# Layer 0's routed experts on 32-token tiles, four experts side by side in the array, with their weights copied to a fixed tile; context LayerNorm scaled on the vector engine

## The chip, the core and the metric

The kernel is one program on one core of a Trainium2 chip. The core has five engines that run their own instruction queues in order and wait for one another by semaphores: TensorE (PE in the profile, with its weight loads as PEld), VectorE (DVE), ScalarE (ACT), GpSimd (POOL) and SyncE (SP, which here only issues DMAs). The metric is the device time of one execution in microseconds; less is better. Times of several executions are given as a median.

## The reference, cut to what matters

The program is a decoder of four layers over `x` of shape (4, 256, 128), which is 1024 tokens of width 128. Each layer adds a self attention, a cross attention to a context of (4, 512, 128), and a feed-forward part. The change touches layer 0's feed-forward part, a mixture of 32 experts with one expert for each token, beside one shared expert:

```python
x = hidden_states.reshape(-1, h)
shared_out = _swiglu(x, shared_gate_w, shared_up_w, shared_down_w)
logits = x @ gate_w
topk_ids = jnp.argmax(logits, axis=-1)
topk_val = jnp.max(logits, axis=-1)
scores = jax.nn.sigmoid(topk_val)[:, None]
xs = x * scores
tokens_per_expert = jnp.zeros((E,), jnp.int32).at[topk_ids].add(1)      # E = 32
order = jnp.argsort(topk_ids)
sorted_x = xs[order]
g = _grouped_mm(sorted_x, routed_gate_w, tokens_per_expert)             # 128 -> 256
u = _grouped_mm(sorted_x, routed_up_w, tokens_per_expert)               # 128 -> 256
d = _grouped_mm(jax.nn.silu(g) * u, routed_down_w, tokens_per_expert)   # 256 -> 128
routed_out = d[inv]
return (shared_out + routed_out).reshape(b, s, h)
```

Layers 1 and 2 have mixtures too (8 experts, two for each token, hidden width 512), and layer 3 an ordinary feed-forward part. Layer 0's cross attention uses the context after a LayerNorm without gains; that LayerNorm is the other thing that the change touches. The inputs are random, with fixed shapes; all arithmetic of the experts is in f32.

## The kernel before

Tokens stand 128 to a tile, eight tiles in all (`NT`), with the tokens on the partitions.

**Layer 0's attention** is woven by a planner that spreads the steps of one unit (a batch and a kind of attention) over the steps of its neighbours. Beside each cross attention unit it places `normalise_context`, which normalises two tiles of the context `cn` at a time. The statistics are taken by DVE (`st`, `mv`, lines L290 and L291), the reciprocal root by POOL (`ve`, `rs`, L296 and L298), and the scaling `(x - mean) * rs` (L304) by POOL too, because `normalise` is called with `G`.

**A mixture** sorts the tokens by expert without sorting them. `blocks_of` counts the tokens of each expert, rounds each count up to whole blocks, and derives three things: `index`, the slot of each token; `token`, the token of each slot; and `at`, for each block, the column at which its expert's weights begin. Every block has 128 slots and one expert. Since each of the 32 experts may leave one block partly empty, the program reserves `size = k * NT + n_e - 1` blocks, which is 8 + 31 = 39 in layer 0 and 16 + 7 = 23 in layers 1 and 2.

`mixture` then runs over the blocks, with four steps that are one block apart:

- `fetch(b)` gathers the 128 rows of block b from DRAM with an indirect DMA on POOL (L1022), five blocks ahead.
- `rows_T(b)` turns them on TensorE (L1029), and ACT copies them to `xbT` (L1031).
- `hidden(b)` multiplies them with the gate and up weights of the block's expert, 512 columns, one f32 matmul that the profile shows as two records (L1042). ACT takes the silu of the gate half (L1136, `sg`), and DVE multiplies it with the up half (L1137, `h`).
- `turned(b)` turns the 256 hidden columns in two transposes (L1052), and DVE copies them to `hT` (L1054).
- `result(b)` multiplies with the down weights in two matmuls of 128 columns, four records (L1063). After every fourth block ACT copies the sums to `ys` (L1078), and SP writes them to `done` in DRAM.

All weights of all experts lie in SBUF (`e0h`: 128 x 16384, and `e0d`: 128 x 8192). TensorE reads them at an address from a register, which its own queue loads from `at` (L1015) ahead of the matmul:

```python
at_h = offset(0, b, (n_e - 1) * n1)
...
T.matmul(p, lhsT=xbT[b], rhs=wh[:, bass.ds(at_h + 512 * i, 512)], ...)
```

The lines are written in the order hidden(b), rows_T(b + 1), fetch(b + 5), turned(b - 1), result(b - 2); a scheduler places them on each engine's queue, and the engines follow that queue strictly.

In `ffn0` the routing comes first (`next(work)`), then the shared expert in two halves of 512 tokens (L1160 gate and up, L1166 silu to `sgs`, L1167 product to `hTs`, L1171 down, L1176 residual), then the block loop. The scheduler mixes the shared expert's matmuls into the routing. After the loop, layer 1 begins with keys for its strided attention (L1268, L1287), while the routed rows are gathered back (L1106) and added to `x` (L1116).

Of the kernel before, what the change touches and what calls it, by code (L numbers as in the profile page):

```python
# [32 lines left out]
P = 128  # L33
# [150 lines left out]
def decoder(ctx: ExitStack, tc: tile.TileContext, dr, out):  # L184
# [78 lines left out]
    slots = const.tile([32, 8], F32, tag="slots", name="slots")  # L263
    V.tensor_scalar(slots, iota[:32, :8], float(P), None, ALU.mult)
    halves = const.tile([P, 2], F32, tag="halves", name="halves")
    G.memset(halves, -0.5)

# [581 lines left out]

    def all_normalised_T(pool, keep=None, tag="pt"):
        xnT = pool.tile([P, NT * P], F32, tag="xnT", name="xnT", bufs=1)
        for b in range(B):
            normalised_T(b, pool, dst=xnT[:, b * S : (b + 1) * S], keep=keep, tag=tag)
        return xnT
# [29 lines left out]
            hot.append(oh)  # L886
        return mx, hot

    def blocks_of(pool, hots, size, widths):

# [23 lines left out]
            )  # L914
        cs = small.tile([32, 1], F32, tag="cs", name="cs")[:n_e]
        V.tensor_copy(cs, count)
        nb = small.tile([32, 8], F32, tag="nb", name="nb")[:n_e]
        V.tensor_scalar(nb, slots[:n_e], cs, None, ALU.is_lt)
        V.tensor_reduce(cs, nb, AX.X, ALU.add)
        nbb = small.tile([32, P], BF16, tag="nbb", name="nbb")[:n_e]  # L920
        V.tensor_scalar(nbb, onesb[:n_e], cs, None, ALU.mult)
# [1 line left out]
        cum = ps("t")[:, :64]  # L923
        T.matmul(cum, lhsT=nbb, rhs=upto_bf[:n_e], start=True, stop=True)
        base = small.tile([P, 32], F32, tag="base", name="base")[:, :n_e]
        V.tensor_scalar(base, cum[:, :n_e], float(P), None, ALU.mult)
        to = pool.tile([P, n, n_e], F32, tag="to", name="to", bufs=1)
        V.tensor_tensor(
            to, rank.rearrange("p (t e) -> p t e", t=n),
# [47 lines left out]
        for i in range(n_w):  # L977
            T.transpose(xp[:1, i * P : (i + 1) * P], ex[:, i : i + 1], ident)
        fill(4, "g")
        at = pool.tile([1, n_w, P], I32, tag="at", name="at", bufs=1)  # L980
        V.tensor_copy(at, xp[:1, : n_w * P].rearrange("p (i b) -> p i b", i=n_w))
        return index, token, at


# [8 lines left out]
        if fetched:  # L993
            fetched.pop(0)()

    def mixture(pool, n_e, hots, weights, rows_, wh, wd, activate, biases=None):

        k = len(hots)  # L1000
        size = k * NT + n_e - 1
        n1, n2 = wh.shape[1] // n_e, wd.shape[1] // n_e
        nh = n2 // P
        sent = dram.tile([NT * P, D], F32, tag=f"sent{n_e}{k}", name="sent")
        done = dram.tile([size * P, D], F32, tag=f"done{n_e}{k}", name="done")
        nc.sync.dma_start(sent.rearrange("(t p) d -> p t d", p=P), rows_)
        index, token, at = blocks_of(pool, hots, size, (n1, n2) if biases is None else (n1, n2, P))
# [5 lines left out]
        def offset(i, b, most):  # L1013

            return nc.values_load(  # L1015
                at[0:1, i, b : b + 1], engines=[mybir.EngineType.PE], min_val=0, max_val=most,
                skip_runtime_bounds_check_because="an expert's number, limited to the last one's",
            )

        def fetch(b):  # L1020
            xb[b] = pool.tile([P, D], F32, tag="xb", name="xb", bufs=ahead + 1)
            G.indirect_dma_start(  # L1022
                out=xb[b], out_offset=None, in_=sent[:, :],
                in_offset=bass.IndirectOffsetOnAxis(ap=token[:, b : b + 1], axis=0),
            )
# [6 lines left out]

        def hidden(b):
            o = [ps("g") for _ in range(0, n1, 512)]
            at_h = offset(0, b, (n_e - 1) * n1)
            for i, p in enumerate(o):
                if biases is not None:
                    T.matmul(
                        p, lhsT=onesb[0:3, :], rhs=biases[0:3, bass.ds(at_h, 512)],
                        start=True, stop=False,  # L1040
                    )
                T.matmul(  # L1042
                    p, lhsT=xbT[b], rhs=wh[:, bass.ds(at_h + 512 * i, 512)],
                    start=biases is None, stop=True,
                )
            h[b] = pool.tile([P, n2], F32, tag="h", name="h", bufs=3)
            activate(pool, h[b], o)

# [7 lines left out]
        def result(b):  # L1056
            g, i = b // 4, b % 4
            if i == 0:
                y[g] = ps("y")
            cols = slice(i * P, (i + 1) * P)  # L1060
            at_d = offset(1, b, (n_e - 1) * n2)
            for c in range(nh):
                T.matmul(  # L1063
                    y[g][:, cols], lhsT=hT[b][:, c * P : (c + 1) * P],
                    rhs=wd[:, bass.ds(at_d + c * P, P)],
                    start=c == 0, stop=c == nh - 1 and biases is None,
                )
            if biases is not None:
                at_b = offset(2, b, (n_e - 1) * P)
                T.matmul(  # L1070
                    y[g][:, cols], lhsT=onesb[0:3, :],
                    rhs=biases[0:3, bass.ds(at_b + n_e * n1, P)],
                    start=False, stop=True,
                )
            if b == groups[g][-1]:
                n = len(groups[g])
                ys = pool.tile([P, 4, D], F32, tag="ys", name="ys")
                A.copy(ys[:, :n, :], y[g][:, : n * P].rearrange("p (n d) -> p n d", n=n))  # L1078
                nc.sync.dma_start(
                    done[4 * g * P : (4 * g + n) * P, :].rearrange("(n p) d -> p n d", p=P),  # L1080
                    ys[:, :n, :],
                )

        yield
        for b in range(ahead):
            fetch(b)
        rows_T(0)
        for b in range(size + 2):
            if b < size:
                hidden(b)  # L1090
            if b + 1 < size:
                rows_T(b + 1)
            if b + ahead < size:
                fetch(b + ahead)
            if 1 <= b <= size:
                turned(b - 1)
            if b >= 2:
                result(b - 2)
# [41 lines left out]
    def ffn0(wh):  # L1140
        with ExitStack() as st:
            pool = expert_pools(st, "ffn0")
            wd = load("e0d", pool=pool)
            xn = pool.tile([P, NT, D], F32, tag="xna", name="xna", bufs=1)
            xnT = all_normalised_T(pool, keep=[xn[:, t, :] for t in range(NT)], tag="t")
            mx, (hot,) = top(pool, logits_of(pool, xnT, gates[:, 0:32], 32, tag="t"), 1)
            score = pool.tile([P, NT], F32, tag="score", name="score", bufs=1)
            A.activation(score, mx[:, :, 0], AF.Sigmoid)
            for t in range(NT):
                G.tensor_scalar(xn[:, t, :], xn[:, t, :], score[:, t : t + 1], None, ALU.mult)  # L1150
            work = mixture(pool, 32, [hot], None, xn, wh, wd, gated(256))
            next(work)

            for c in range(2):
                hT = pool.tile([P, 2, 512], F32, tag="hTs", name="hTs", bufs=1)
                for ic in range(2):
                    gu = []
# [24 lines left out]
    def ffn1(wh, wd, ahead):  # L1182
        with ExitStack() as st:
# [6 lines left out]
            work = mixture(pool, 8, hots, small_softmax(pool, mx), xn, wh, wd, gated(512))  # L1190
            next(work)
            next(work)
            wq3.extend(ternary_weights(ahead, w3f))
# [13 lines left out]
    def ffn2():  # L1207
        with ExitStack() as st:
# [30 lines left out]
            def activate(pool_, h, o):  # L1239
# [4 lines left out]
                    V.tensor_scalar(h, o[0], 0.0, None, ALU.max)  # L1244

            work = mixture(
                pool, 8, hots, [best[:, i] for i in range(2)], xn, wh, wd, activate, bias
            )
            next(work)
            next(work)  # L1250
# [811 lines left out]
```

## Time and profile before

| what | value |
|---|---|
| median of the three runs | 1609.93 us |
| the three runs | 1610.73, 1606.98, 1609.93 us |
| the profiled execution, its own time | 1610.05 us |
| its span, from first to last instruction | 1608.2 us |
| mean granted clock of TensorE | 0.916 of full speed |
| busy share of the span: PE, DVE, ACT, POOL | 86%, 51%, 45%, 19% |
| chain of work that ended last: PE, DVE, ACT, POOL | 72%, 11%, 7%, 4% |
| hidden matmuls of the three mixtures in that chain (L1042) | 7% |

The shares are averages over stages that have different limits, so a stage is read from its own stretch. Layer 0's attention runs from the start to about 278 us, the routing and the shared expert to about 307 us, the block loop of layer 0 from 309 to 387 us, and layer 1 follows. In the groups of instructions the first number after the bar is the busy time in us, the second the mean duration of one in ns, and after the next bar stands the time that the engine was idle just before them and who ended it. A clock of 1.00 is full speed.

### The profile page before, as it was taken

The page shows a single profiled execution, that of the slowest core. Times are in us where ns is not written, and L with a number is a line of the kernel's source. Part 1 is how long each engine was busy: PE and PEld are TensorE (multiplying, and loading weights), DVE is VectorE, ACT ScalarE, POOL GpSimd, SP SyncE. Part 2 cuts the span into 40 slices and gives each one's busy share as a digit, 9 for nine tenths or more (in the row PEclk, how much of TensorE's full clock was granted, in tenths as well). Part 3 has the DMA queues.
Part 4 walks back from the last instruction along what each step waited for, and adds up shares of the span by engine and source line. Part 5 has one row for each costly group of instructions (what it writes and reads, how often), then busy time and mean ns, then how long its engine had stood idle before and what let it go on. Part 6 is the DMA issues. An engine that isn't in the chain of part 4 may idle for free.

```text
span 1608.2 us, 27001 instructions
## 1 busy us (share of the span) xinstructions
PE 1383.7 (86%) x10108; PEld 733.2 (46%) x10108; DVE 816.0 (51%) x2690; ACT 721.6 (45%) x1428; POOL 312.5 (19%) x440
## 2 busy tenths in 40 slices
PE   4998998698786899888999999999596699999963
PEld 3543333465344465645455554455364344333321
DVE  5676661444564344764434543441433557765336
ACT  0544656233652334256666756766121044344431
POOL 5235100452312224200000000000232522211000
PEclk8999999798798899999999999999698599999985
DMA  8000001232040314150110000000312000000000
GB/s 313 1 1 1 2 1 54 84 68 57 7 202 14 105 39 150 53 183 14 49 45 14 27 1 1 1 1 1 130 45 52 27 1 2 1 2 1 1 2 12
DMA packets 38754, 70.98 MB, mean 44 GB/s; under 512 B 5477, under 2 KB 22159, under 8 KB 36703
## 3 DMA queue, kind: packets, MB, share of 16 engines
q1 hardware_dynamic: 33474, 51.39, 9.1%
q0 software_dynamic: 4000, 8.20, 2.5%
q10 hardware_dynamic: 1152, 9.67, 1.5%
q8 instruction: 82, 1.34, 0.3%
q14 instruction: 46, 0.38, 0.1%
HBM read 51.06 MB, written 18.18 MB: 43 GB/s over the span
## 4 chain that ended last, share of the span: by engine, by line
PE 72%; DVE 11%; ACT 7%; POOL 4%; issue 3%; DMA 2%; another core or an unknown queue 0%; SPq 0%; ACTq 0%; POOLq 0%; DVEq 0%
PE s L538 7%; PE g L1042 7%; PE o L574 7%; PE s L473 6%; PE o L1789 6%; PE s L1769 5%; PE f L1718 4%; PE y L1063 4%; PE s L525 3%; PE f L1704 2%; PE s L532 2%; PE t L1052 2%; PE f L1674 2%; DVE mx L480 2%; PE s L1762 2%
## 5 line engine op out<-in xcount | busy, mean ns | idle before, releaser
L473 PE MATMUL s<-kc,qm 32*128 32x256 f32 (+1 forms) x1024 | 217.3, 559 | 14.0 <-POOL qm L428 8.4
L555 ACT ACTIVATE pr<-s 128x512 f32<-128x512 f32 x256 | 137.9, 596 | 185.1 <-PE s L538 183.6
L538 PE MATMUL s<-qm,kc 32*128 32x512 f32 (+1 forms) x896 | 207.5, 605 | 0.0
L296 POOL TENSOR_SCALAR ve<-mv 128x2 f32<-128x2 f32 (+1 forms) x56 | 12.7, 228 | 758.4 <-DVE mv L291 694.1
L1729 ACT ACTIVATE ss<-ss,ntop 128x768 f32<-128x768 f32 x128 | 118.6, 928 | 85.6 <-DVE ntop L1727 85.3
L480 DVE TENSOR_REDUCE mx<-s 128x1 f32<-128x512 f32 (+1 forms) x192 | 122.5, 685 | 65.2 <-PE s L538 50.5
L574 PE MATMUL o<-pr,v 128*32 128x256 f32 (+1 forms) x1792 | 145.6, 391 | 9.0 <-ACT os L580 4.1
L1723 DVE CUSTOM_DVE_ANT_0 ss<-f,n 128x512 f32<-128x512 f32 x128 | 83.4, 689 | 74.5 <-PE f L1718 74.3
L473 PEld LDWEIGHTS s<-kc,qm 32*128 32x128 f32 x1024 | 88.1, 204 | 68.9 <-issue 19.5
L484 DVE CUSTOM_DVE_ANT_0 junk<-s,nmif 128x512 bf16<-128x512 f32 x128 | 83.0, 688 | 54.0 <-PE s L473 53.5
L1789 PE MATMUL o<-pr,v 128*64 128x256 f32 x768 | 108.8, 395 | 0.0
L1022 POOL DMA_INDIRECT xb<-sent,token x85 | 81.0, 952 | 140.5 <-PE t L1029 63.8
L557 ACT ACTIVATE pr<-s,n 128x512 f32<-128x512 f32 x128 | 80.1, 690 | 60.4 <-PE s L538 40.1
L1769 PE MATMUL s<-qT,kT 64*128 64x256 f32 x768 | 105.3, 390 | 0.0
L574 PEld LDWEIGHTS o<-pr,v 128*32 128x32 f32 x1792 | 40.4, 109 | 117.5 <-issue 88.6
L1776 ACT ACTIVATE pr<-s,n 128x512 f32<-128x512 f32 x128 | 80.2, 678 | 22.0 <-PE s L1769 21.9
L428 POOL TENSOR_SCALAR qm<-q,consts 128x256 f32<-128x256 f32 x64 | 58.6, 932 | 145.9 <-ACT q L425 115.6
L532 PE MATMUL s<-mT,selg 12*128 12x256 bf16 x768 | 80.6, 276 | 4.2 <-DVE mT L274 1.2
L1054 DVE COPY hT<-t 128x512 f32<-128x512 f32 (+1 forms) x85 | 48.1, 566 | 68.8 <-PE t L1052 64.3
L1711 DVE CUSTOM_DVE_ANT_0 ss<-f,nought 128x256 f32<-128x256 f32 x128 | 46.8, 421 | 60.9 <-PE f L1704 60.7
L1718 PE MATMUL f<-kT,qT 64*128 64x512 f32 x256 | 76.6, 624 | 0.1
L1789 PEld LDWEIGHTS o<-pr,v 128*64 128x64 f32 x768 | 47.8, 136 | 60.4 <-issue 23.5
(404 smaller groups left out, 2513.8 us busy)
## 6 DMA issues: line engine op xcount, KB each, us to landing
e0h<-in_e0h SPq DMA_DIRECT2D x8, 1024.0 KB
kd<-ahead SPq DMA_DIRECT2D x20, 256.0 KB
vd<-ahead SPq DMA_DIRECT2D x20, 256.0 KB
kT<-kd SPq DMA_DIRECT2D x20, 256.0 KB
v<-vd SPq DMA_DIRECT2D x5, 1024.0 KB
done<-ys SPq DMA_DIRECT2D x19, 256.0 KB
e0d<-in_e0d SPq DMA_DIRECT2D x1, 4096.0 KB
e1h<-in_e1h ACTq DMA_DIRECT2D x1, 4096.0 KB
```

Source lines behind the costliest of these rows:

```text
L473: T.matmul(sc[:, i, :], lhsT=u.qm[r, g + i, qt * P : (qt + 1) * P], rhs=u.kc[r, :], start=u.row_mask is None, stop=True,)
L480: V.tensor_reduce(u.mx[:, qt, j, g : g + per], sc, AX.X, ALU.max)
L532: T.matmul(sc[:, i, :], lhsT=selg[r, gp + i, :], rhs=u.mT[r, :], start=u.cols_mask is None and i == 0, stop=False,)
L538: T.matmul(sc, lhsT=u.kc[r, kt * P : (kt + 1) * P], rhs=u.qm[r, gp : gp + 2, first:], start=u.clip, stop=True,)
L555: A.activation(dst, sc, AF.Exp)
L574: T.matmul(u.po[gp][32 * j : 32 * j + 32, i, first:], lhsT=u.v[:, kt, 4 * j + gp + i, :], rhs=u.pr[gp, kt, j][:, i, first:], start=kt + i ...
L1042: T.matmul(p, lhsT=xbT[b], rhs=wh[:, bass.ds(at_h + 512 * i, 512)], start=biases is None, stop=True,)
L1718: T.matmul(sc[h], lhsT=qT[u, c][hrow[h], qt * P : (qt + 1) * P], rhs=kT[u, c][hrow[h], :SK], start=True, stop=True,)
L1723: V.tensor_tensor_reduce(ss[qt][h][:, :SK], sc[h], neg1[:, b * SK : (b + 1) * SK], 1.0, -3e38, ALU.add, ALU.max, accum_out=mx[:, qt, h, 1:2],)
L1729: A.activation(ss[qt][h], ss[qt][h], AF.Exp, bias=ntop[:, qt, h, c : c + 1], accum_out=total[:, qt, h, c : c + 1],)
L1769: T.matmul(sc[h][:, i, :], lhsT=kT[u, c][hrow[h], kt * P : (kt + 1) * P], rhs=qT[u, c][hrow[h], :], start=False, stop=i == 1,)
L1789: T.matmul(po[u, g][hrow[h], i, :], lhsT=v[u][:, kt, n * hd : (n + 1) * hd], rhs=pr[u, g, kt, h][:, i, :], start=kt + i == 0, stop=kt + i ...
```

## The change

The change has three parts.

1. A mixture takes a new argument `per`, the tokens of one expert tile. Layer 0 passes 32, layers 1 and 2 pass 128. With 32, a block of 128 slots holds four tiles (`m = 4`), each with an expert of its own, and the number of blocks becomes `ceil((k * NT * m + n_e - 1) / m)` = ceil(63 / 4) = 16. For each block DVE copies the gate and up weights of its four experts to a tile `wbh` (four copies of 128 x 512, `weights_in`, one block ahead), and ACT the down weights to `wbd` (four copies of 128 x 256, `weights_out`). The registers with the offsets are loaded on DVE's and ACT's queues, four by one load. The matmuls of a block are then four with 32 columns of tokens each, which write 32 partitions each: 4 instead of 1 in `hidden`, 8 instead of 2 in `result`. With `per` 128 the matmuls read the weights by register as before; in layer 2, which has biases, `hidden` loads the same offset once for the bias and once for the weights.
2. In `ffn0` four tiles get other places: `xnT` and `hTs` share the three buffers of `wbd` (so `hTs` alternates between buffers), and `sgs` uses the two buffers of `ys`.
3. `normalise_context` calls `normalise` without `G`, so DVE does the 16 scalings of `cn`.

```diff
-    def blocks_of(pool, hots, size, widths):
+    def blocks_of(pool, hots, per, size, widths):
...
-        nb = small.tile([32, 8], F32, tag="nb", name="nb")[:n_e]
-        V.tensor_scalar(nb, slots[:n_e], cs, None, ALU.is_lt)
+        nb = small.tile([32, NT * P // 32], F32, tag="nb", name="nb", bufs=1)[:n_e, : NT * P // per]
+        V.tensor_scalar(
+            nb, iota[:n_e, : NT * P // per], float(per), cs, ALU.mult, ALU.is_lt
+        )
...
-        V.tensor_scalar(base, cum[:, :n_e], float(P), None, ALU.mult)
+        V.tensor_scalar(base, cum[:, :n_e], float(per), None, ALU.mult)
...
-        at = pool.tile([1, n_w, P], I32, tag="at", name="at", bufs=1)
-        V.tensor_copy(at, xp[:1, : n_w * P].rearrange("p (i b) -> p i b", i=n_w))
+        m = P // per
+        at = pool.tile([1, P // m, n_w, m], I32, tag="at", name="at", bufs=1)
+        V.tensor_copy(at, xp[:1, : n_w * P].rearrange("p (i g j) -> p g i j", i=n_w, j=m))
...
-        size = k * NT + n_e - 1
+        m = P // per
+        size = -(-(k * NT * m + n_e - 1) // m)
+        tiles_ = [slice(j * per, (j + 1) * per) for j in range(m)]
...
+        def offsets(i, b, engine):
+            _, values = nc.values_load_multi_w_load_instructions(
+                at[0:1, b, i, :], engines=[engine], min_val=0, max_val=(n_e - 1) * widths[i],
+                ...
+            )
+            return values
+
+        wb = {}
+
+        def weights_in(b):
+            w = wb[0, b] = pool.tile([P, m, n1], F32, tag="wbh", name="wbh", bufs=2)
+            for j, v in enumerate(offsets(0, b, mybir.EngineType.DVE)):
+                V.tensor_copy(w[:, j, :], wh[:, bass.ds(v, n1)])
+
+        def weights_out(b):
+            w = wb[1, b] = pool.tile([P, m, n2], F32, tag="wbd", name="wbd", bufs=3)
+            for j, v in enumerate(offsets(1, b, mybir.EngineType.Activation)):
+                A.copy(w[:, j, :], wd[:, bass.ds(v, n2)])
+
+        def taken(i, b, n):
+            if per == P:
+                (v,) = offsets(i, b, mybir.EngineType.PE)
+                all_w = (wh, wd)[i]
+                return [(slice(0, P), lambda c: all_w[:, bass.ds(v + c, n)])]
+            return [
+                (r, lambda c, j=j: wb[i, b][:, j, c : c + n]) for j, r in enumerate(tiles_)
+            ]
...
-            at_h = offset(0, b, (n_e - 1) * n1)
+            blocks = taken(0, b, 512)
             for i, p in enumerate(o):
                 if biases is not None:
+                    (at_h,) = offsets(0, b, mybir.EngineType.PE)
...
-                T.matmul(
-                    p, lhsT=xbT[b], rhs=wh[:, bass.ds(at_h + 512 * i, 512)],
-                    start=biases is None, stop=True,
-                )
+                for r, w in blocks:
+                    T.matmul(
+                        p[r], lhsT=xbT[b][:, r], rhs=w(512 * i), start=biases is None, stop=True,
+                    )
...
+            blocks = taken(1, b, P)
             for c in range(nh):
-                T.matmul(
-                    y[g][:, cols], lhsT=hT[b][:, c * P : (c + 1) * P],
-                    rhs=wd[:, bass.ds(at_d + c * P, P)],
-                    start=c == 0, stop=c == nh - 1 and biases is None,
-                )
+                for r, w in blocks:
+                    T.matmul(
+                        y[g][r, cols], lhsT=hT[b][:, c * P : (c + 1) * P][:, r], rhs=w(c * P),
+                        start=c == 0, stop=c == nh - 1 and biases is None,
+                    )
...
+        if per < P:
+            weights_in(0)
         rows_T(0)
         for b in range(size + 2):
+            if per < P and b + 1 < size:
+                weights_in(b + 1)
+            if per < P and b < size:
+                weights_out(b)
             if b < size:
                 hidden(b)
...
-            work = mixture(pool, 32, [hot], None, xn, wh, wd, gated(256))
+            work = mixture(pool, 32, 32, [hot], None, xn, wh, wd, gated(256))
...
-                hT = pool.tile([P, 2, 512], F32, tag="hTs", name="hTs", bufs=1)
+                hT = pool.tile([P, 2, 512], F32, tag="wbd", name="hTs", bufs=3)
...
-                    sg = pool.tile([P, 512], F32, tag="sgs", name="sgs", bufs=1)
+                    sg = pool.tile([P, 512], F32, tag="ys", name="sgs")
...
     def normalise_context(b, i):
         two = [cn[:, NKT * b + i, :], cn[:, NKT * b + i + 1, :]]
-        normalise(two, two, G)
+        normalise(two, two)
```

More of the change, by code (lines that the diff above doesn't have):

```diff
@@ L261, in decoder @@
     V.tensor_scalar(gscale, gmask, SCALE8, None, ALU.mult)
-    slots = const.tile([32, 8], F32, tag="slots", name="slots")
-    V.tensor_scalar(slots, iota[:32, :8], float(P), None, ALU.mult)
     halves = const.tile([P, 2], F32, tag="halves", name="halves")
@@ L848, in fill, with all_normalised_T @@
             spare.pop(0)(tag)
-    def all_normalised_T(pool, keep=None, tag="pt"):
-        xnT = pool.tile([P, NT * P], F32, tag="xnT", name="xnT", bufs=1)
+    def all_normalised_T(pool, keep=None, tag="pt", like=("xnT", 1)):
+        xnT = pool.tile([P, NT * P], F32, tag=like[0], name="xnT", bufs=like[1])
         for b in range(B):
@@ L994, in settle, with mixture @@
             fetched.pop(0)()
-    def mixture(pool, n_e, hots, weights, rows_, wh, wd, activate, biases=None):
+    def mixture(pool, n_e, per, hots, weights, rows_, wh, wd, activate, biases=None):
         k = len(hots)
-        size = k * NT + n_e - 1
+        m = P // per
+        size = -(-(k * NT * m + n_e - 1) // m)
+        tiles_ = [slice(j * per, (j + 1) * per) for j in range(m)]
         n1, n2 = wh.shape[1] // n_e, wd.shape[1] // n_e
@@ L1006, in mixture @@
         nc.sync.dma_start(sent.rearrange("(t p) d -> p t d", p=P), rows_)
-        index, token, at = blocks_of(pool, hots, size, (n1, n2) if biases is None else (n1, n2, P))
+        widths = (n1, n2) if biases is None else (n1, n2, P)
+        index, token, at = blocks_of(pool, hots, per, size, widths)
         groups = [range(b, min(b + 4, size)) for b in range(0, size, 4)]
@@ L1011, in mixture @@
         ahead = 5
-        def offset(i, b, most):
-            return nc.values_load(
-                at[0:1, i, b : b + 1], engines=[mybir.EngineType.PE], min_val=0, max_val=most,
+        def offsets(i, b, engine):
+            _, values = nc.values_load_multi_w_load_instructions(
+                at[0:1, b, i, :], engines=[engine], min_val=0, max_val=(n_e - 1) * widths[i],
                 skip_runtime_bounds_check_because="an expert's number, limited to the last one's",
             )
+            return values
[16 more added lines that the diff above has]
+            ]
         def fetch(b):
@@ L1060, in result @@
             cols = slice(i * P, (i + 1) * P)
-            at_d = offset(1, b, (n_e - 1) * n2)
+            blocks = taken(1, b, P)
             for c in range(nh):
-                T.matmul(
-                    y[g][:, cols], lhsT=hT[b][:, c * P : (c + 1) * P],
-                    rhs=wd[:, bass.ds(at_d + c * P, P)],
-                    start=c == 0, stop=c == nh - 1 and biases is None,
-                )
+                for r, w in blocks:
[3 more added lines that the diff above has]
+                    )
             if biases is not None:
-                at_b = offset(2, b, (n_e - 1) * P)
+                (at_b,) = offsets(2, b, mybir.EngineType.PE)
                 T.matmul(
                     y[g][:, cols], lhsT=onesb[0:3, :],
-                    rhs=biases[0:3, bass.ds(at_b + n_e * n1, P)],
-                    start=False, stop=True,
+                    rhs=biases[0:3, bass.ds(at_b + n_e * n1, P)], start=False, stop=True,
                 )
@@ L1144, in ffn0 @@
             xn = pool.tile([P, NT, D], F32, tag="xna", name="xna", bufs=1)
-            xnT = all_normalised_T(pool, keep=[xn[:, t, :] for t in range(NT)], tag="t")
+            xnT = all_normalised_T(
+                pool, keep=[xn[:, t, :] for t in range(NT)], tag="t", like=("wbd", 3)
+            )
             mx, (hot,) = top(pool, logits_of(pool, xnT, gates[:, 0:32], 32, tag="t"), 1)
@@ L1189, in ffn1 @@
             mx, hots = top(pool, logits_of(pool, xnT, gates[:, 32:40], 8, tag="t"), 2)
-            work = mixture(pool, 8, hots, small_softmax(pool, mx), xn, wh, wd, gated(512))
+            work = mixture(
+                pool, 8, P, hots, small_softmax(pool, mx), xn, wh, wd, gated(512)
+            )
             next(work)
@@ L1246, in ffn2 @@
             work = mixture(
-                pool, 8, hots, [best[:, i] for i in range(2)], xn, wh, wd, activate, bias
+                pool, 8, P, hots, [best[:, i] for i in range(2)], xn, wh, wd, activate, bias
             )
```

## The prediction, on record before the changed kernel was run

> **What bounds the kernel now.** I read the page's 40 slices first, for which stretches TensorE fills, then the busy time by stretch around layer 0's experts, then their timeline.
>
> ```profile
> core 0: us, PE busy (x) PEld busy (x) DVE busy (x) ACT busy (x) POOL busy (x), PEclk, DMA share, GB/s
> 304.00:314.00 10.00, 6.78 (x34) 4.13 (x33) 3.15 (x8) 2.28 (x8) 7.21 (x8) 1.00 0.19 40
> 314.00:345.00 31.00, 27.43 (x125) 17.73 (x125) 10.30 (x28) 9.10 (x31) 14.83 (x16) 0.89 0.28 61
> 345.00:380.00 35.00, 34.99 (x177) 23.10 (x177) 15.03 (x40) 13.43 (x45) 15.14 (x16) 1.00 0.35 70
> ```
>
> From 345 to 380 us TensorE is busy 34.99 of 35.00 us while DVE and ACT are under half: the loop over 39 blocks is TensorE's. One period of it in the timeline:
>
> ```profile
> 347.06 1.12 PE L1042 MATMUL g<-e0h,xbT 128*128 x2
> ...
> 348.01 0.27 PE L1029 MATMUL t<-consts,xb 128*128 128x128 f32 x1
> ...
> 348.12 0.38 PE L1052 MATMUL t<-consts,h 128*128 128x128 f32 x2
> ...
> 348.34 0.61 PE L1063 MATMUL y<-e0d,hT 128*128 x4
> ...
> 348.84 1.12 PE L1042 MATMUL g<-e0h,xbT 128*128 x2
> ```
>
> From start to start it is 1.78 us, of which the three transposes take about 0.33 (0.11 from one to the next) and the four down records 0.44 to 0.50. 39 x 1.78 = 69.4 us. The loop lasts from 309.4 (first hidden matmul) to 387.1 us: 77.7 us. The 8 us over are the start, some microseconds at half clock, a TensorE pause of some 3.6 us before 319.5 whose cause the profile does not know, and the last block's way out.
>
> **What the Trainium skill says.** "TensorEngine Tiling (Array Packing)", Tiling Modes: with 32 columns to a tile the array works as four independent tiles, and a change of mode drains the engine. The trace agrees: in attention eight 32-column matmuls of 256 columns (16 records) start 1.00 us before the next work, where each streams for 0.43 us by L1042's pace (512 columns in 0.86 in layer 1's loop): 3.4 us in sequence. "VectorE: DVE Perf Modes", Mode 2×_2P: an f32 copy from SBUF to SBUF runs at two elements a cycle. It agrees: L1883 takes 0.43 us for 512 elements, copies of 512 from PSUM 0.69. "SBUF — State Buffer", A bandwidth-pool intuition that's wrong: such a copy keeps GpSimd from writing the descriptors of its own DMAs until it ends. No run here shows that yet; layer 0's gathers are such DMAs. "TensorE: Matmul & The Clock Gate", What's actually happening: a TensorE that is not busy falls to half clock. The stretch at 0.89 agrees.
>
> **The change, part by part.**
>
> Blocks. 39 (8 + 31) become 16, from 8x4 + 31 = 63 tiles of 32 tokens over 4. A block keeps one gather, three transposes, one silu, one product and one hT copy; 23 of each go.
>
> TensorE for one new block. Lines for columns:
>
> ```profile
> 257.72 1.07 PE L574 MATMUL o<-pr,v 128*32 128x256 f32 x16
> 258.72 0.42 PE L532 MATMUL s<-mT,selg 12*128 12x256 bf16 x8
> ...
> 387.10 4.48 PE L1268 MATMUL s<-cT,w1x 128*32 128x128 f32 x32
> ```
>
> In L574 each column tile does four records in 1.00 us, 0.25 for 256 columns, so about 0.04 over the 0.21 of streaming. Hidden: two records of 512 columns in each tile, 2 x 0.47 = 0.95. Down: four records of 128 columns in each tile, between 4 x (0.107 + 0.04) = 0.6 and 0.9 if loads do not overlap (L1268, successive in one column tile, shows 0.14 to 0.22 a record); I take 0.75. Transposes 0.33 and three changes of tiling at some 0.1 (an estimate, the gaps seen between forms): 2.3 us.
>
> DVE for one new block. The durations, as groups (busy us, mean ns | idle before) of the loop and then as two lines' instructions (least/median/most ns):
>
> ```profile
> L1054 DVE COPY hT<-t 128x256 f32<-128x256 f32 x39 | 16.6, 425 | 45.2 <-PE t L1052 40.8 <-remote 4.4
> L1137 DVE TENSOR_TENSOR h<-sg,g 128x256 f32<-128x256 f32 x39 | 16.0, 411 | 3.7 <-ACT sg L1136 3.2 <-issue 0.5
> ...
> L1136 ACT ACTIVATE sg<-g 128x256 f32<-128x256 f32 x39 | 15.0, 384 | 47.1 <-PE g L1042 40.3 <-remote 5.0 <-issue 1.7
> ...
> L1031 ACT COPY xbT<-t 128x128 f32<-128x128 f32 x39 | 10.0, 260 | 4.2 <-PE t L1029 4.2
> ```
>
> ```profile
> L1883 DVE TENSOR_SCALAR wt<-wt x2: 427/427/427, 621.9 to 623.4; 128x512 f32<-128x512 f32 x2
> L1015 PEldq TENSOR_LOAD <-at x193: 293/299/546, 308.3 to 1230.8; - x193
> ```
>
> Four copies of 128x512 by 0.40 = 1.6 (0.43 less a little overlap), product 0.41, hT 0.43: 2.45. The load of the four offsets moves onto DVE's own queue: 0.30, plus about 0.1 until its first address is set (0.4 on TensorE's queue). It stands behind the hT copy, which still runs 0.43 when the queue goes on, so I take 0.1 of it; the ends are 0 and 0.9, if the four address operations (0.12 apart on TensorE's queue) show too. 2.55, from 2.45 to 3.35.
>
> ACT for one new block. Four copies of 128x256 from SBUF: a silu of 256 takes 0.38, and L1459 at 512 from SBUF (0.63) is 0.03 over the same from PSUM, so 0.41, in a row some 0.37: 1.5. Silu 0.38, xbT 0.26, a quarter of ys (0.59) 0.15, loads 0.2 to 0.5: 2.5 to 2.8.
>
> Three engines are within 0.3 us of another, and all are in order. What is queued behind the new copies: on DVE the product, for which TensorE's transposes wait, and on ACT the silu, for which the product waits. TensorE runs ahead (wbh two deep, weights fetched a block early, g four banks), so none of these waits closes a cycle within one block. **I take 2.8 us a block**, a little over the slowest; 2.35 (TensorE alone) and 3.4 are the ends.
>
> The first weights. The order that the changed kernel is built in puts DVE's first load behind the shared expert's last product and residual. Four copies (1.6) then stand ahead of the first hidden matmul, where before it waited for a gather (token at 304.2, landed at 308.2). Smaller routing masks (L949, L955, L959: 0.48 + 0.48 + 0.29 for 312 columns, now 128) save 0.6, double-buffered hTs and sgs save a little on the shared expert, whose products now come ahead of the routing's end. I keep 309 us for the first hidden matmul, give or take 1.5. Waits on the wbd slots that xnT and hTs used end with the shared expert, before ACT needs them.
>
> Loop after: 16 x 2.8 = 44.8, plus 2.2 for the last block (silu, product, transposes, hT, down), plus 1 for half clock or half of an unknown pause: 48. Against 77.7: **-30 us**, from 16 x 2.35 + 2 - 77.7 = -38 to 16 x 3.4 + 6 - 77.7 = -17.
>
> Other queues. POOL issues 16 gathers of 0.95 instead of 39; even at three times the time they keep up with 2.8 a block, five ahead. SP issues 4 instead of 10 writes of done and is no bound. Nothing after the loop has a date of its own: the last write of done, its gathers and layer 1's keys all start from the loop's end, so what is saved reaches the end. w1x (issued at 384.1, waited for 0.9 us at 387.0) can only come relatively earlier.
>
> Context LayerNorm. 16 scalings leave POOL (16 x 0.80 = 12.8 us) for DVE (16 x 0.30 = 4.8). In 110 to 195 us no TensorE wait is on cn's scaling but 1.6 us the other way (POOL for TensorE); DVE waited 4.0 for POOL's cn and has 25 of 85 us free. On the other side each pair must now wait on DVE for POOL's rs (about 1 us after mv, more behind POOL's qm, 3.6), with max reductions that drain TensorE's banks queued behind it. I take 0; the ends are -3 and +6.
>
> Layer 2's experts. hidden() now loads the offset twice: 23 more loads of 0.3 to 0.4 us on TensorE's queue. That queue runs about 1 us ahead there (the address of L1042 is set at 1185.04, its matmul runs at 1186.29), so 0; at most 23 x 0.4 = +9.
>
> **The rivals.** (1) As above. For: the wait lists show DVE and ACT idle for TensorE 40 us each in this loop. (2) The copies become the bound at 3.4 to 4: exposed addresses, the shared port that gathers and copies fight for, or a TensorE that falls to half clock (its 2.3 become some 4.2). 16 x 3.8 + 4 - 77.7 = -13: 1597. For: no run shows a register-addressed copy on DVE or ACT. Against: half clock would make TensorE 100% busy, and half-clock stretches that are 100% busy last 3.4 to 6.8 us in this trace. (3) **Slower**: the four column tiles do not overlap. Hidden 4 x 0.85 = 3.4, down 8 x 0.21 = 1.7, transposes 0.33, tiling 0.2: 5.6 x 16 + 3 - 77.7 = +15: 1625. It decides from (77.7 - 2.2) / 16 = 4.7 us a block. For: L1268's records stand one after another. Against: those share one column tile, L574 takes turns between four as the new loop does. (4) The time saved is swallowed at layer 1's start by some transfer: 1607. Nothing in the chain after 387 us says so.
>
> **How the numbers follow.** The profiled execution took 1610.05 us (span 1608.2), 0.1 from the median 1609.93. 1610 - 30 = 1580. Chances: (1) 0.75, (2) 0.18, (3) 0.04, (4) 0.03. The likeliest gives 1580; the low end is -38, -3 for the context and -3 for start and pause: 1566; the high end holds (2)'s middle, 1597. 0.3% (5 us) is about what a measurement of this kernel can tell from no change. Only (3), and a part of (4), are not faster: faster 0.93, same 0.03, slower 0.04.
>
> **What would show it.** Right: the expert loop lasts 45 to 52 us, L1042's place holds 8 records in under 1.1 us, DVE's copies take 0.40 to 0.45, DVE and ACT are over 85% busy in the loop, and layer 2's period stays 2.87. Wrong: copies of 0.6 or more, a period over 3.3, TensorE at half clock for long, layer 0's attention longer by over 5 us, or column records that start 0.4 apart.

## The result, and the profile after

| kernel | median, us | runs | lowest to highest | ratio to before, 95% interval |
|---|---|---|---|---|
| before | 1610.33 | 4 | 1606.98 to 1616.84 | |
| changed | 1591.19 | 4 | 1587.75 to 1597.34 | 0.9881 [0.9837, 0.9924] |

The changed kernel is 19 us faster. The prediction said 1580, with 1566 to 1597 as its range. The two profiled executions (spans 1608.2 and 1586.0, the changed one timed at 1587.75, the fastest of its four) differ by 22.2 us, and the landmarks of the timeline say where. An "update of x" is the instruction that adds the result of one attention unit to the residual `x` (L613 before, L610 after); "attention ends" is the start of the last one in layer 0. The last column is how much longer or shorter the stage that ends at this landmark became.

| | before, us | changed, us | change of the stage |
|---|---|---|---|
| first update of x | 68.3 | 70.4 | +2.1 |
| attention ends | 278.9 | 288.3 | +7.3 |
| first hidden matmul | 309.4 | 321.0 | +2.2 |
| last down matmul ends | 387.1 | 366.5 | -32.2 |
| layer 1's loop begins | 545.8 | 522.7 | -2.5 |
| layer 1's loop ends | 620.5 | 598.5 | +1.1 |
| layer 2's loop begins | 1163.7 | 1140.3 | -1.4 |
| layer 2's loop ends | 1231.8 | 1208.9 | +0.5 |
| span ends | 1608.2 | 1586.0 | +0.7 |

So the loop over blocks gave 32 us, and some 12 us were lost ahead of it: 2 before the first update of x, which nothing here ties to an edit, 7 in the attention and 2 after it.

**The loop.** Busy time by stretch of the changed kernel (stretch, its length, then busy us with the instructions counted of each engine, granted clock, DMA share, GB/s):

```profile
core 0: us, PE busy (x) PEld busy (x) DVE busy (x) ACT busy (x) POOL busy (x), PEclk, DMA share, GB/s
321.00:328.00 7.00, 6.49 (x29) 1.27 (x28) 3.04 (x9) 3.69 (x12) 5.48 (x6) 0.57 0.22 52
...
335.00:350.00 15.00, 13.28 (x163) 5.15 (x162) 13.00 (x38) 10.76 (x36) 4.35 (x4) 1.00 0.24 42
```

Before, TensorE filled 34.99 of 35 us. Now it fills 13.28 of 15 (89%), DVE 87% and ACT 72%: no engine is full, so waits must make up the rest of the period. One period in the timeline (start, length, engine, line, work, and in brackets the idle time before it with its releaser):

```profile
343.18 0.64 PE L1096 MATMUL y<-wbd,hT 128*32 128x128 f32 x16
343.29 0.42 DVE L1086 COPY hT<-t 128x256 f32<-128x256 f32 x1 [0.23 <-PE t L1084]
...
343.82 1.44 DVE L1034 COPY wbh<-e0h 128x512 f32 x4
343.95 1.33 ACT L1039 COPY wbd<-e0d 128x256 f32 x4 [1.19 <-PE y L1096]
...
344.02 1.06 PE L1075 MATMUL g<-wbh,xbT 128*32 128x512 f32 x8
...
345.18 0.26 ACT L1062 COPY xbT<-t 128x128 f32<-128x128 f32 x1
345.34 0.38 ACT L1173 ACTIVATE sg<-g 128x256 f32<-128x256 f32 x1
...
345.49 0.44 PE L1084 MATMUL t<-consts,h 128*128 128x128 f32 x2 [0.41 <-issue]
345.76 0.42 DVE L1174 TENSOR_TENSOR h<-sg,g 128x256 f32<-128x256 f32 x1 [0.50 <-ACT sg L1173]
...
345.86 0.64 PE L1096 MATMUL y<-wbd,hT 128*32 128x128 f32 x16
```

The hidden place (the stretch of one block's gate and up matmuls, L1075) with its 8 records lasts 1.06 us, about as long as the old place with 2 records over all 128 columns (1.12): the four column tiles work at the same time. `y` are the down products. ACT stood idle for 1.19 us until the down products ended at 343.8, and then copied for 1.33 us, with xbT's copy and the silu behind the copies. The chain of waits from 335 to 350 us, by engine and line, says the same:

```profile
by line: PE g L1075 20.2%; PE y L1096 20.0%; ACT wbd L1039 17.8%; PE t L1084 14.1%; issue 11.2%; PE t L1060 5.6%; ACT ys L1109 4.2%; ACT xbT L1062 3.3%; ACT sg L1173 3.0%; ACTq L1039 2.1%; ACTq L1022 2.1%; ACTq L1062 0.1%
```

DVE, the second busiest engine, is not in this chain at all. ACT, at 72%, is. A chain in a trace is still an inference; experiments 4 to 6 test it.

**The attention.** TensorE computes scores `s` (L464, L529), and DVE takes the maxima of their rows, `mx` (L477); TensorE's later scores wait for that. What DVE waited for between 116 and 206 us in the changed kernel, and TensorE (total, times, longest):

```profile
DVE cn L301 <- POOL rs L295: 8.6, 4, 3.8
```

```profile
PE s L529 <- DVE mx L477: 5.6, 2, 5.3
PE s L464 <- DVE mx L477: 4.7, 1, 4.7
```

The lines of the kernel before:

```profile
DVE mv L291 <- POOL cn L304: 4.0, 2, 2.9
```

```profile
PE s L467 <- DVE mx L480: 4.2, 1, 4.2
...
PE s L532 <- DVE mx L480: 0.6, 2, 0.3
```

And the timeline of POOL and of DVE around the first of these waits:

```profile
119.39 0.72 POOL L295 TENSOR_TENSOR rs<-ve,halves 128x2 f32<-128x2 f32 x1
120.22 1.58 POOL L301 TENSOR_SCALAR xn<-x,mv,rs 128x128 f32<-128x128 f32 x2
121.77 0.86 POOL L347 TENSOR_TENSOR x<-x,rows 128x128 f32<-128x128 f32 x2
122.61 0.23 POOL L293 TENSOR_SCALAR ve<-mv 128x2 f32<-128x2 f32 x1
122.92 0.71 POOL L295 TENSOR_TENSOR rs<-ve,halves 128x2 f32<-128x2 f32 x1
```

```profile
119.61 0.30 DVE L288 BATCH_NORM_AGGREGATE mv<-st 128x2 f32<-128x6 f32 x2
123.67 0.60 DVE L301 TENSOR_SCALAR cn<-cn,mv,rs 128x128 f32<-128x128 f32 x2 [3.75 <-POOL rs L295]
...
125.18 1.28 DVE L477 TENSOR_REDUCE mx<-s 128x1 f32<-128x512 f32 x2
```

POOL does the rows' own normalisation (rs, xn, and the bias added to x) before it comes to the context's root at 122.92. DVE's scaling stands in DVE's queue ahead of the max reductions, so DVE does nothing for 3.75 us, the reductions come at 125.18, and TensorE's scores wait for them. The granted clock is 0.50 from 123 to 130 us and again from 153 to 159, after the second such wait.

### The profile page after: what moved, and what is told of

Same layout as the page of the kernel before. It is cut to its first block, busy times and chain, and to the rows that moved or that the text cites. A ratio compares the mean times of both kernels' runs of the same rounds, so it can differ in the third digit from the quotient of the medians.

```text
span 1586.0 us, 26992 instructions
## 1 busy us (share of the span) xinstructions
PE 1351.7 (85%) x10188; PEld 699.6 (44%) x10189; DVE 824.2 (52%) x2723; ACT 726.2 (46%) x1440; POOL 277.9 (18%) x401
## 4 chain that ended last, share of the span: by engine, by line
PE 69%; DVE 11%; ACT 7%; POOL 5%; issue 5%; DMA 2%; ACTq 0%; SPq 0%; POOLq 0%; DVEq 0%
PE o L571 7%; PE s L535 7%; PE s L470 6%; PE o L1830 6%; PE s L1810 5%; PE g L1075 5%; PE f L1759 4%; PE s L522 3%; PE y L1096 2%; PE f L1745 2%; PE s L529 2%; PE f L1715 2%; PE s L1803 2%; PE s L343 2%; POOL back L1143 2%
## 5 line engine op out<-in xcount | busy, mean ns | idle before, releaser
L470 PE MATMUL s<-kc,qm 32*128 32x256 f32 (+1 forms) x1024 | 222.1, 574 | 13.9 <-POOL qm L425 8.4
L477 DVE TENSOR_REDUCE mx<-s 128x1 f32<-128x512 f32 (+1 forms) x192 | 122.6, 685 | 68.7 <-PE s L535 52.0
L293 POOL TENSOR_SCALAR ve<-mv 128x2 f32<-128x2 f32 (+1 forms) x56 | 12.7, 227 | 767.9 <-DVE mv L288 703.5
L529 PE MATMUL s<-mT,selg 12*128 12x256 bf16 x768 | 80.9, 277 | 8.4 <-DVE mx L477 6.1
L1053 POOL DMA_INDIRECT xb<-sent,token x62 | 60.5, 976 | 125.2 <-PE t L1060 68.6
L1752 DVE CUSTOM_DVE_ANT_0 ss<-f,nought 128x256 f32<-128x256 f32 x128 | 46.8, 421 | 60.2 <-PE f L1745 60.1
L1810 PEld LDWEIGHTS s<-qT,kT 64*128 64x128 f32 x768 | 68.2, 192 | 6.2 <-issue 0.2
```

Of the source, the lines that this page charges most:

```text
L470: T.matmul(sc[:, i, :], lhsT=u.qm[r, g + i, qt * P : (qt + 1) * P], rhs=u.kc[r, :], start=u.row_mask is None, stop=True,)
L477: V.tensor_reduce(u.mx[:, qt, j, g : g + per], sc, AX.X, ALU.max)
L529: T.matmul(sc[:, i, :], lhsT=selg[r, gp + i, :], rhs=u.mT[r, :], start=u.cols_mask is None and i == 0, stop=False,)
L1810: T.matmul(sc[h][:, i, :], lhsT=kT[u, c][hrow[h], kt * P : (kt + 1) * P], rhs=qT[u, c][hrow[h], :], start=False, stop=i == 1,)
```

## The experiments

Theory W: the context's scaling on DVE waits for POOL and holds up the max reductions. Its rival R: the later attention comes from elsewhere (clock, start). Theory C: the loop's period is a cycle through the three buffers of down weights and ACT's queue. Its rivals V and T: DVE's or TensorE's own work. All landmarks in one table (us; "attention" is from the first to the last update of x, "loop" from the first hidden to the last down matmul):

| kernel | first update | attention | loop | span | ratio to before |
|---|---|---|---|---|---|
| before | 68.3 | 210.6 | 77.7 | 1608.2 | |
| changed | 70.4 | 217.9 | 45.5 | 1586.0 | 0.9881 [0.9837, 0.9924] |
| experts alone | 71.6 | 210.4 | 46.8 | 1583.6 | 0.9821 [0.9792, 0.9849] |
| context alone | 70.4 | 220.9 | 76.8 | 1620.7 | 1.0043 [1.0028, 1.0059] |
| late scaling | 68.2 | 203.9 | 45.5 | 1570.7 | 0.9782 [0.9755, 0.9808] |
| four down buffers | 71.7 | 210.4 | 38.5 | 1573.6 | 0.9772 [0.9745, 0.9798] |
| both | 73.0 | 204.1 | 38.1 | 1569.0 | 0.9723 [0.9703, 0.9744] |
| half of DVE's copies | 71.3 | 210.3 | 47.4 | 1582.8 | |
| half of ACT's copies | 69.1 | 210.8 | 40.9 | 1571.8 | |
| blocks of 64 | 71.5 | 210.5 | 57.7 | 1600.7 | 0.9909 [0.9894, 0.9924] |

The attention's length repeats well: the six kernels that scale on POOL show 210.3 to 210.8 us, the two that scale late 203.9 and 204.1. The first update varies from 68.2 to 73.0 us. Context alone and before have the same program in that stretch and still differ by 2.1 us, so none of this column is put down to an edit.

**1. The experts alone** (the changed kernel, with the scaling on POOL again):

```diff
-        normalise(two, two)
+        normalise(two, two, G)
```

> The experts' part of the change alone: the context's scaling is back on POOL, the rest is the changed kernel. TensorE's, ACT's and SP's order of instructions is that of the changed kernel; only DVE's and POOL's differ. Theory W (the context's scaling on DVE waits for POOL and holds up the max reductions behind it): the last update of x in layer 0's attention comes at 279 us of the span as in the kernel before, the loop over blocks still lasts 45 to 46 us, and the time is 1610 - 30 = 1580 us, 0.981 of the kernel before, some 9 us below the changed kernel. Theory R (the 9 us are no effect of the scaling but of the first 70 us, where the changed kernel was already 2 us late, and of where TensorE's half clock happens to fall): the attention still ends at 285 us or later, and the time stays at 0.987 to 0.989.

Measured: 1585.37 us median, 0.9821. The attention lasts 210.4 us, as before the change, and the loop 46.8, a little over the 45 to 46 expected. The experts' part is thus worth 27 us by the medians and 29 by the ratio (1612.76 is the median of before beside experiments 1 to 4). The end of the attention came at 282.0, not 279, but 3.3 us of that were there at the first update. Where W and R speak of the attention's length, W holds.

**2. The context alone** (the kernel before, with the scaling on DVE):

```diff
-        normalise(two, two, G)
+        normalise(two, two)
```

> The context LayerNorm's part alone: the kernel before with the context's scaling on DVE, 128-token blocks and no copies of weights. Theory W: the attention of layer 0 ends 8 to 10 us later, at 287 to 289 us, with two waits of DVE on rs of over 3 us each ahead of max reductions in the first half of the cross-attention, and the time is 1618 to 1620 us, 1.005 to 1.006 of the kernel before. Theory R: within 0.2% of the kernel before, 1607 to 1613 us, with DVE's waits on rs taken up by TensorE's reserve. The prediction's own value was 0, its upper end +6.

Measured: 1620.15 us, 1.0043 [1.0028, 1.0059], so +7 us, a little under W's 1.005 and outside R's 0.2%. The attention is 10.3 us longer in the profiled execution, which was 2.3 us slower than the median. DVE's and TensorE's waits from 116 to 206 us, and the stretch from 120 to 160 us:

```profile
DVE cn L304 <- POOL rs L298: 8.5, 4, 3.7
```

```profile
PE s L532 <- DVE mx L480: 5.6, 2, 5.3
PE s L467 <- DVE mx L480: 4.7, 1, 4.7
```

```profile
120.00:160.00 40.00, 28.30 (x222) 10.47 (x221) 23.95 (x73) 11.36 (x20) 13.21 (x27) 0.79 0.00 1
```

TensorE waits 10.3 us for DVE's maxima where the kernel before waited 4.8. The clock records of these traces hold only 1.00 and 0.50. The mean of 0.79 in 40 us is thus some 0.21 x 2 x 40 = 17 us at half clock; before, that stretch had 0.91, which is 7 us:

```profile
120.00:160.00 40.00, 34.01 (x329) 13.76 (x329) 27.13 (x77) 18.27 (x31) 24.36 (x40) 0.91 0.01 1
```

5.5 us more waiting, and up to half of 10 us more at half clock, would cover the 10.3 us. That is an estimate: what half clock cost was not separated. The experts alone had 0.96 in that stretch, less half clock than before, and their attention is no shorter (210.4).

**3. Late scaling** (the changed kernel; still DVE, but the scaling of a pair is put off while newer pairs come, pinned in DVE's queue, and what is left is scaled before layer 1 turns the context):

```diff
-        normalise(two, two)
+        scale_waiting(2)
+        waiting.append((statistics(two, like="c"), two))
...
     def turn_context(b):
+        scale_waiting()
```

`scale_waiting(n)` scales the oldest pairs until n are left, and `like="c"` gives the context's statistics tiles of their own.

> The changed kernel with the context's scaling still on DVE, but each pair scaled one attention unit later than its statistics (which keep their place), so that rs lies ready; TensorE's and ACT's order is that of the changed kernel, and the scalings' 16 x 0.30 us stay DVE's. Theory W: no wait of DVE on rs over 0.5 us, the attention ends at 278 to 281 us, and the time is 1579 to 1582 us, 0.981 to 0.983, as with the scaling on POOL. Rival D (it is DVE's added 4.8 us of work, in a stretch where its max reductions feed TensorE, and not the wait): the attention still ends at 284 us or later, and the time is 1585 us or more. Theory R: as D.

Measured: 1577.77 us, 0.9782 [0.9755, 0.9808], 0.010 under the changed kernel. The attention lasts 203.9 us. All that remains of DVE's list of waits from 116 to 206 us, and the stretch from 120 to 160 us:

```profile
DVE mx L477 <- PE s L535: 23.7, 30, 1.6
DVE x L610 <- PE s L606: 0.9, 1, 0.9
```

```profile
120.00:160.00 40.00, 38.42 (x397) 15.24 (x397) 29.09 (x73) 22.29 (x38) 11.09 (x20) 1.00 0.01 1
```

DVE now waits for TensorE's scores alone, and TensorE is busy 38.42 of 40 us at full clock. The edit did more than put each pair one unit off, though. All its scalings (count, then least/median/most ns, first and last start):

```profile
L1990 DVE TENSOR_SCALAR cn<-cn,mv,rs x16: 335/340/343, 192.9 to 380.4; 128x128 f32<-128x128 f32 x16
```

No context tile is scaled before 192.9 us, on any engine; the last six scalings come from 379.2 us on, in layer 1, and the statistics of the last two pairs moved to 193.7 and 211.7. So the stretch that had lost time is rid of the work as well as of the wait, and this run alone does not refute rival D. The stretches from one update of x to the next tell more (us; in brackets the scalings on DVE in them; before, POOL did 4, 8 and 4 in the first three of these):

| stretch | before | changed | late scaling |
|---|---|---|---|
| third to fourth update | 18.5 | 26.4 (4) | 18.7 (0) |
| fourth to fifth | 48.4 | 49.5 (8) | 41.6 (0) |
| fifth to sixth | 37.3 | 37.3 (4) | 37.5 (4) |
| sixth to seventh | 35.7 | 35.7 (0) | 35.6 (4) |
| seventh to eighth | 23.3 | 21.7 (0) | 23.2 (2) |

Where scalings on DVE wait for nothing, the stretch is as long as before within 0.2 us: four in the changed kernel, ten in this one. Where they wait 3.75 us, four scalings of 0.34 us come with 7.9 us more. (The 21.7 of the changed kernel's last stretch is not explained.) Rival D would have to get 7.9 us from 1.4 us of work, so the wait is much the likelier cost. A kernel that keeps the work in those stretches and takes away the wait alone was not run.

W's number was too small, too. It foresaw the old attention back (210 us); it is 6.7 us shorter than that, and all of it in the fourth to fifth update. There the kernel before had its own version of the wait, DVE's statistics for tiles that POOL's scalings still held (4.0 us) and TensorE 4.2 us behind it; here no engine scales in that stretch. What is shown is the worth of having the scaling out of it. Whether POOL could do it late as well was not tried.

**4. Four down buffers** (the experts alone, with buffers of the loop traded):

```diff
-        ahead = 5
+        ahead = 5 if per == P else 4
...
-            w = wb[1, b] = pool.tile([P, m, n2], F32, tag="wbd", name="wbd", bufs=3)
+            w = wb[1, b] = pool.tile([P, m, n2], F32, tag="wbd", name="wbd", bufs=4)
...
```

The room comes from one buffer less each of xbT, h and sg in layer 0's loop, and of xb by `ahead`.

> The experts' part alone with four instead of three buffers for the down weights' copies on ACT (the room comes from one buffer less each of sg, h, xbT and xb in layer 0's loop). Theory C (the period of 2.6 us is a cycle: down products free a buffer, ACT's four copies of 1.33 us follow, then xbT's copy and the silu, for which DVE's product and TensorE's transposes wait, then the down products): the copies no longer wait for y, the period falls to 2.3 to 2.45 us, the loop to 41 to 43 us, 3 to 5 us below the experts' part with three buffers. Rival V (DVE's own work bounds the period: 1.44 of copies, 0.41 and 0.42 of product and hT, 0.35 of load): the loop stays at 45 to 46 us, and so does the time, within 1 us. Rival T (TensorE, 89% busy in the loop): the same as V, or 1 us at most.

Measured: 1575.37 us, 0.9772, 10 us under the experts alone, more than C's 3 to 5. The loop lasts 38.5 us, and from the fourth block on the period is 2.20 us. Busy time, and one block's down products, copies and hidden place in the timeline:

```profile
324.00:346.00 22.00, 22.00 (x274) 8.78 (x270) 20.32 (x58) 19.31 (x64) 7.15 (x7) 1.00 0.25 49
```

```profile
329.41 0.64 PE L1096 MATMUL y<-wbd,hT 128*32 128x128 f32 x16
329.55 0.70 ACT L1039 COPY wbd<-e0d 128x256 f32 x2
...
330.24 1.06 PE L1075 MATMUL g<-wbh,xbT 128*32 128x512 f32 x8
```

ACT copies while the down products still run, and TensorE is full again: 22.00 of 22. V and T are both out as bounds of the changed kernel, since neither engine got less work here. TensorE's own 2.20 us is the bound only of this kernel.

**5. Half of DVE's copies** (the experts alone; two of the four gate and up copies are left out, and tiles 2 and 3 read those of tiles 0 and 1):

```diff
-            for j, v in enumerate(offsets(0, b, mybir.EngineType.DVE)):
+            for j, v in enumerate(offsets(0, b, mybir.EngineType.DVE)[:2]):
```

> The experts' part alone (three down buffers) with two instead of four gate and up copies per block on DVE: tiles 2 and 3 use the copies of tiles 0 and 1, so two of four tiles have another tile's weights. DVE's work per block falls by 2 x 0.34 = 0.68 us. Theory C (the period of 2.2 to 3.0 us is the cycle through the down buffers and ACT's queue): the loop stays at 45 to 47 us, and DVE's product waits for the silu the longer for it, by about 0.6 us a block. Rival V (DVE's queue bounds the period): the loop falls by up to 16 x 0.47 us to TensorE's 2.20 a block, to 38 to 40 us.

Measured, one execution: the loop lasts 47.4 us, no shorter than with all copies (46.8). From 330 to 350 us:

```profile
330.00:350.00 20.00, 18.06 (x231) 8.36 (x231) 12.11 (x32) 15.25 (x51) 4.01 (x5) 1.00 0.32 58
```

DVE's share falls to 61% and nothing is gained. V falls.

**6. Half of ACT's copies** (the same with the down copies):

```diff
-            for j, v in enumerate(offsets(1, b, mybir.EngineType.Activation)):
+            for j, v in enumerate(offsets(1, b, mybir.EngineType.Activation)[:2]):
```

> The mirror of the half of DVE's copies: the experts' part alone, still three down buffers, with two instead of four down copies per block on ACT (tiles 2 and 3 use the down weights of tiles 0 and 1, so two of four tiles have another tile's weights). ACT's work per block falls by 2 x 0.31 = 0.62 us, DVE's stays. Theory C (the cycle down products, a buffer free, ACT's copies, xbT, silu): the cycle falls below TensorE's 2.20 us, and the loop from 46.8 to 38 to 40 us. A rival to C (what helped the kernel with four buffers was not the fourth buffer but one less of sg, h, xbT or xb): the loop stays at 45 to 47 us, since those are as before here.

Measured, one execution: the loop lasts 40.9 us, 5.9 less, with three buffers still and sg, h, xbT and xb untouched, so the loop can get its gain without the trade in those that experiment 4 made. From 325 to 345 us:

```profile
325.00:345.00 20.00, 19.54 (x243) 7.66 (x241) 19.12 (x56) 12.12 (x38) 4.13 (x4) 1.00 0.25 45
```

Most blocks take 2.20 us; each fourth, in which ACT also copies ys (0.59), takes 2.5, which is why 38 is not reached. The less busy of the two copying engines held the loop, as C says.

**7. Blocks of 64** (experts alone, `mixture(pool, 32, 64, ...)` for `mixture(pool, 32, 32, ...)`):

> The experts' part alone with blocks of 64 tokens, two to a block of 128 in array columns of 64: 16 + 31 = 47 blocks, so 24 instead of 16 rounds of the loop, each with half of the copies on DVE and ACT. Theory P (TensorE's own work, 2.20 us a block with four tiles, falls only by half of the 16 down records, and the down buffers' cycle shrinks by ACT's 0.67 us to about TensorE's time): 1.9 to 2.2 us a block, the loop 50 to 56 us, the time 4 to 9 us over the experts' part with blocks of 32. Rival K (the copies are what a block costs): about 1.6 us a block, the loop 42 to 45 us, the time 2 to 4 us under it.

Measured: 1598.04 us, 0.9909, 12.7 us over the experts alone, and a loop of 57.7 us. Both were wrong: K in its sign, P in its size (50 to 56 us, 4 to 9 over). One block of the timeline:

```profile
336.42 1.08 PE L1075 MATMUL g<-wbh,xbT 128*64 128x512 f32 x4
337.43 0.44 PE L1084 MATMUL t<-consts,h 128*128 128x128 f32 x2
337.80 0.66 PE L1096 MATMUL y<-wbd,hT 128*64 128x128 f32 x8
338.39 0.33 PE L1060 MATMUL t<-consts,xb 128*128 128x128 f32 x1
```

Half as many records take the same time: 1.08 against 1.06, and 0.66 against 0.64. P had counted on fewer down records being shorter. TensorE's block costs 2.23 us here and 2.20 with four tiles (experiment 4); 24 x 2.23 = 53.5, and the slower blocks at the start and two later ones of 2.64 make up the rest. So tiles of 32 gain over tiles of 64 by the number of blocks, 16 for 24, and not by cheaper blocks.

**8. Both cures** (late scaling and four down buffers in the changed kernel):

> The changed kernel with both cures: the context's scaling on DVE one attention unit later, and four buffers for the down weights' copies (one less of sg, h, xbT and xb). If the two are independent, as theories W and C say, the gains add: attention from the first update of x at its end in 204 us, the loop in 38 to 39 us with a period of 2.20, the ratio 0.9782 + 0.9772 - 0.9821 = 0.973, some 1569 us. Rival (one eats the other, for instance since DVE's later scalings move into the routing or POOL's work changes place): 0.976 or more.

Measured: 1567.04 us (1565.72 to 1573.56), 0.9723 [0.9703, 0.9744], with 204.1 us of attention and a loop of 38.1. The two gains add: 0.973 was expected if they do. This version beats both kernels: 45 us under its 1611.98 of before.

## Why the prediction was right or wrong

- **The loop, -30: right in size.** It is -32.2 in the pair of profiles; the experts alone gained 27 to 29 us in time. Four column tiles do overlap, as the prediction read out of L574 and as the Trainium skill has it ("TensorEngine Tiling (Array Packing)", Tiling Modes). Rival 3 (slower) needed 4.7 us a block; between the hidden starts at 333.38 and 354.33 there are 8 blocks of 2.62. The terms: hidden 0.95 foretold and 1.06 measured, down 0.75 and 0.64, DVE's copy 0.40 and 0.34 from one to the next, ACT's 0.37 and 0.31.
- **What sets the period: wrong.** The prediction took the slowest engine plus a little, 2.8, and wrote that "none of these waits closes a cycle within one block". It went through wbh, g and the early fetch, but not through wbd, the tile of the down weights: block b's copies, block b-1's and the down products of b-2 hold all three buffers, so the next copies wait for those products, and xbT's copy and the silu stand behind them on ACT. Without the cycle the answer was TensorE's 2.3, measured 2.20. Its 2.8 came near 2.62 by a margin that stood in for a mechanism; that was luck. "DVE and ACT over 85% busy" came true for DVE alone.
- **DVE's load of offsets, 0.1 of 0.345 us exposed: right.** In the timeline the hT copy ends at 343.71 and the first weight copy starts at 343.82.
- **Copies against gathers:** the Trainium skill warns that such copies hold up GpSimd's descriptors ("SBUF — State Buffer", A bandwidth-pool intuition that's wrong). Here it is little, and the measurement decides: the issue of a gather went from a median of 946 to 1044 ns, 10%, and with half of DVE's copies it is 947. From the third block on TensorE waited for no gather, with five blocks ahead and with four.
- **The context LayerNorm, 0 with ends -3 and +6: wrong, the step that failed.** Alone it costs 7 us (1.0043), a little beyond the upper end, and the prediction's own sign of being wrong, an attention longer by over 5 us, came (+7.3). The prediction named the wait ("each pair must now wait on DVE for POOL's rs") and what stands behind it, and then set it at nothing because DVE was idle 25 of 85 us. Mean idle time is no cover for one wait of 3.75 us: POOL's xn and x add (2.4 us) stood ahead of the root and the max reductions behind the scaling, and the granted clock was 0.50 in the stretch that followed.
- **The text ahead of the prediction has one error that belongs here.** It says that layer 0's cross attention uses the normalised context. It does not: `context_T` turns the raw `cn`, and the normalised tiles are first read by `turn_context` in layer 1, at 396.4 us (L1991). So the last scalings, at 198.7 us, had almost 200 us to spare and the first more, and the third experiment could put them off at no cost that its landmarks show.
- **First hidden matmul 0 (+-1.5): +2.2 after the end of the attention.** Kernels with the new experts show 31.4 to 33.0 us there, context alone 32.1 and before 30.5, so part of it is not the experts' part. Nor is it the copies ahead of the first matmul, which the prediction named: from `token` (L967), which lets the gathers start, to the first hidden matmul it is 5.2 to 5.3 us in all ten kernels, and in the changed one the fourth copy ended at 319.36, 1.6 us before that matmul at 320.98. The 2.2 us arise ahead of `token`, in the routing and the shared expert; what makes them stays open.
- **Layer 2's second load of the offset, 0: right,** +0.5 us in its loop. After layer 0's loop, 0 was foretold: -1.6 in sum.
- **Half clock in the block loop:** the prediction argues against rival 2 that half-clock stretches which TensorE fills last 3.4 to 6.8 us. In the trace of before, those that it fills last 3.4 (267.1 to 270.4, for one); the fullest of 6.8 is filled to 91% (499.2 to 505.9).
- **The sum.** 1610 - 30 + 0; in place of 0, +7 for the context and about +2 for the start give 1589, against 1591.2 measured. That 1591 lies within 1566 to 1597 owes something to luck: the upper end was set for dearer copies, which did not come (0.43 us each), and what used it up was the context's wait.

## What to carry to other kernels

Before a wait is priced at nothing, follow both queues at that place: what stands ahead of the releaser on its engine, and what stands behind the waiter on the other. For a loop in steps, count for each buffered tile the blocks that hold it at once; where that number equals its buffers, producer and consumer form a cycle, and the engine to relieve is the one in the cycle, not the busiest. And look up who reads a result first: work with a late reader can be put where nobody waits.

## What the runs showed of the hardware

For these shapes narrow column tiles cost no more time than wide ones: four tiles of 32 columns, two of 64 or one of 128 take 1.06, 1.08 and 1.12 us for 512 f32 columns each. A copy from SBUF to SBUF at an address from a register took 0.43 us on DVE for 128x512, like the 0.43 of L1883's pass over a fixed tile (0.34 from one to the next in a row), and 0.40 on ACT for 128x256 (0.31); the load of four offsets takes 0.345 us on DVE's queue and 0.31 on ACT's, beside other work.
